# Sorting edges on one core: counts of a group kept in DRAM, order within a column by a rising line and Sign, bias rows of the experts made ahead of their loop

## The chip, the cores and the metric

The kernel runs on one core of a Trainium2 chip. The metric is device time in microseconds (us) of the whole program, the median of several executions; lower is better. A core has five engines with a queue of instructions each: TensorE (PE, matrix products; PEld is its loading of the stationary matrix), VectorE (DVE), ScalarE (ACT), GpSimd (POOL) and SyncE (SP, which here only starts DMAs). Engines work in order within their queue and wait for one another by semaphores. On-chip memory is SBUF (128 partitions) and, for the results of matmuls, PSUM. POOL starts the indirect DMAs, which gather or scatter 128 rows by a list of indices.

## What is computed

A graph layer over 3125 nodes (256 wide), a four-layer transformer with linear attention over the same nodes, and a mixture of four experts routed by a graph attention:

```python
xn = _layernorm(x)
x = x + gnn(xn, edge_attr_64, src, dst, ...) + mix(xn[None], ...)[0]
x = x + ffn(_layernorm(x)[None], ..., L0_ffn_edge_index)[0]

# gnn: messages of 103125 edges (dst is sorted), summed at the receiver, then an MLP
messages = concatenate([nodes[senders], edges], -1) @ W_message
agg = segment_sum(messages, receivers, num_segments=3125)
...
# ffn: attention over 65536 edges (not sorted) and a loop at each node
e = leaky_relu(a_src[src] + a_dst[dst], 0.2)
ee = exp(e - segment_max(e, dst)[dst])
alpha = ee / (segment_sum(ee, dst)[dst] + 1e-16)
agg = segment_sum(h[src] * alpha[:, :, None], dst) + b_gat
scores = _layernorm(agg, ...).reshape(M, 4, 4).mean(1)
topk_s, topk_i = top_k(scores, 2); w = softmax(topk_s)
for ei in range(4):
    g = where(topk_i == ei, w, 0).sum(-1)
    out = out + g[..., None] * (gelu(x @ W1[ei] + b1[ei]) @ W2[ei] + b2[ei])
```

The segment sums and maxima of the last part need the 65536 edges in the order of their receiver, so the kernel sorts them. That sort is what most of the change is about.

## The kernel before

**Layout.** The nodes are 25 tiles of 128 rows, in chunks of four tiles. The 65536 edges to be sorted lie as 128 partitions x 512 columns (TE); a group is 8 columns (GC), so there are 64 groups. A receiver number is cut in two digits: `lo`, its low five bits (32 values), and `hi`, the rest (up to 128 values). A place in the sorted list is: the number of edges with a smaller receiver, plus those with the same receiver in an earlier column, plus those with the same receiver in the same column and an earlier partition.

**Count pass** (`count_group`, L664 to L667, 64 jobs). DVE makes one-hot tiles of both digits with one comparison each (`one_hot`, L657: 128x1024 for `hi`, 128x256 for `lo`). For each column PE multiplies the two (L667) and adds all 512 products up in one PSUM table of 128 x 32 (`table`, part of `sums_ps`): how many edges there are of each receiver. `starts` (L677 to L691) turns the table into the first place of each receiver, which is stored to DRAM (`start_d`) and split into two fp16 parts, `near` and `rest` (`split`, L671 and L672), since one fp16 number can't hold it.

**Place pass** (`place_group`, L693 to L740, 65 jobs: a group's last step, the look, is done one job late). For each group:
1. SP loads `hr`, the high digits of the group's edges broadcast to all partitions (L698, two buffers); DVE compares them with the partition number: `ohT` (L700), the one-hot transposed.
2. DVE makes both one-hots again (L657). PE puts `rest` into column 0 of a PSUM tile (identity x `rest`, L705) and the counts of the eight columns beside it (L707).
3. DVE runs a scan along the columns (L709), PSUM to SBUF: `run`, the start of each receiver at each column. `base` (L712) is the state after the group and is split anew (L671, L672), for the next group.
4. For the order within a column PE puts a mask (identity x `mask`, 0 for a smaller partition and -1 otherwise, L720) into PSUM and adds `ohT` x `ohT` (L722); ACT's Relu (L723) leaves 1 where an earlier partition has the same high digit: `earlier`.
5. One job later PE adds up `ohT` x `near`, `ohT` x `run` and `earlier` x `oh_lo` (the look, 24 matmuls, L734); DVE picks each edge's own value by its low one-hot (L736, L737). Every fourth group `laid` turns 32 columns of numbers into `place`.

POOL then scatters each edge's source to its place (`send`, L750, 512 scatters), and later reads the sorted list.

**What sets the order of the work around it.** The sort is done beside other work. `jobs` is a list of closures with an estimated time, and `beside(us)` (L766) runs the next ones when the transformer's code grants it time: the count groups within layer 0, the ends of the message sums next, the place groups spread over layers 1 to 3. Throughout that time POOL gathers the rows of the message edges (L467, 806 gathers of 128 rows into three buffers `m_run`), DVE adds them up along a partition (L479), and SP stores a full buffer (`run_d`, L484) and loads the edge attributes for the next use of that buffer (L446). Within these bounds a scheduler orders the instructions of each queue; the order in the queues is fixed when the program is built. SP's queue holds all of the loads and stores named here, so each stands behind those ahead of it.

**Experts** (`expert`, L1271). For each of four experts the weights are loaded, then `bias_rows` (L139 to L152) makes the output bias ready for a matmul: a load of the bias to 65 partitions, a fill with zeros and eleven small operations on DVE, which split the fp32 bias into three bf16 rows. Its tiles have one buffer each for all experts. PE adds the bias by a matmul with ones (L1290). Beside the experts POOL gathers the sorted edges' rows (L1192) and DVE works on them in chunks.

Of the kernel before, what the change touches and what calls it, by code (L numbers as in the profile page):

```python
# [18 lines left out]
P = 128  # L19
# [23 lines left out]
GC = 8  # L43
SRC = 4096
# [13 lines left out]
def kernel(ctx: ExitStack, tc: tile.TileContext, a: dict, out: bass.AP):  # L58
# [80 lines left out]
    def bias_rows(pool, vec, name, **k):  # L139

        full = pool.tile([65, D], F32, name=f"{name}_full", **k)
        nc.sync.dma_start(full, vec.rearrange("(o n) -> o n", o=1).to_broadcast([65, D]))
        parts = pool.tile([65, 2, D], BF16, name=f"{name}_parts", **k)
        part = pool.tile([65, D], BF16, name=f"{name}_part", **k)
# [191 lines left out]
    V.tensor_copy(hi, d)  # L336
    hi_f = tmp2.tile([P, TE], F32, name="hi_f")
    V.tensor_copy(hi_f, d)
# [18 lines left out]
    mask = const.tile([P, P], F16, name="mask")  # L357
    V.tensor_scalar(mask, before, -1.0, None, op0=ALU.add)
# [17 lines left out]
    sums_ps = px.tile([P, LO + 2 * NT], F32, name="sums_ps")  # L376

    table, whole_ps, first_ps = sums_ps[:, :LO], sums_ps[:, LO:LO + NT], sums_ps[:, LO + NT:]
# [282 lines left out]
    def one_hots(t):  # L661
        return one_hot(t, hi, P, "oh_hi", 2), one_hot(t, lo, LO, "oh_lo", 3)

    def count_group(t):  # L664
        ohh, ohl = one_hots(t)
        for i in range(GC):
            T.matmul(table, ohh[:, :, i], ohl[:, :, i], start=t + i == 0, stop=t + i == TE - 1, skip_group_check=True)  # L667

    def split(x, near, rest):

        V.tensor_copy(near, x)  # L671
        V.tensor_tensor(rest, x, near, op=ALU.subtract)  # L672

    def parts():
        return (so.tile([P, LO], F16, name="near", bufs=3), so.tile([P, LO], F16, name="rest", bufs=2))

    def starts():  # L677
        cnt2 = so.tile([P, LO], F32, name="cnt2", tag="base")
        V.tensor_copy(cnt2, table)
# [10 lines left out]
        places.append(parts())  # L690
        split(cum2, *places[0])  # L691

    def place_group(t):  # L693

        late = looks.pop() if looks else None
        if t < TE:
            hr = so.tile([P, GC, P], F16, name="hr", bufs=2)
            nc.sync.dma_start(hr.rearrange("p t e -> p (t e)"), row_h[t // GC:t // GC + 1, :].to_broadcast([P, P * GC]))  # L698
            ohT = so.tile([P, GC, P], F16, name="ohT", bufs=2)
            V.tensor_scalar(ohT, hr, bin_p, None, op0=ALU.is_equal)  # L700
            ohh, ohl = one_hots(t)
            near, rest = places.pop()

            cnt = pg.tile([P, LO, GC + 1], F32, name="ps_g")
            T.matmul(cnt[:, :, 0], ident_h, rest, start=True, stop=True)  # L705
            for i in range(GC):
                T.matmul(cnt[:, :, i + 1], ohh[:, :, i], ohl[:, :, i], start=True, stop=True)  # L707
# [9 lines left out]
            for i0 in range(0, GC, 4):  # L717
                ps = pt.tile([P, 4, P], F32, name="ps_t")
                for i in range(4):
                    T.matmul(ps[:, i, :], ident_h, mask, start=i == 0, stop=False, skip_group_check=True)  # L720
# [819 lines left out]
```

## Time and profile before

| what | us |
| --- | --- |
| median of the runs shown (3718.54 to 3738.28) | 3732.21 |
| the profiled execution: time | 3741.95 |
| the profiled execution: span, first to last instruction | 3740.2 |
| PE busy, 10851 matmuls | 2260.1 (60%) |
| POOL busy | 1782.3 (48%) |
| DVE busy | 1478.6 (40%) |
| ACT busy | 1028.8 (28%) |
| message gathers, L467, x806 | 802.7 busy, 996 ns each |
| scatters of the sort, L750, x512 | 494.2 busy, 965 ns each |
| row gathers beside the experts, L1192, x400 | 382.1 busy, 955 ns each |
| sum-ups of the messages, L479, x805 | 437.6 busy, 544 ns each |

A row of a group of instructions reads: line, engine, operation, what it writes and reads by the program's names, the shape, how many; then the busy time and the mean duration of one in ns; then how long the engine was idle just before these instructions, and what ended most of that time. "issue" is time for which the profile shows no wait, "remote" is a release that it can't name. A row of a stage reads: the window and its length, the busy time of each engine with the number of instructions, the clock that TensorE was granted (1 is full speed), the mean busy share of the 16 DMA engines, and GB/s. Over the span the granted clock was 0.762, and 350.22 MB were moved.

By time: 0 to 45 us is preparation, 45 to about 400 layer 0 with the count groups, up to 2745 the place groups (from about 500), 45 to 1690 the message gathers, 1647 to 2822 the scatters, 2900 to 3610 the experts with the edge chunks.

### The profile page before, as it was taken

What the parts mean: (1) busy time and instruction counts of PE and PEld (TensorE: products, weight loads), DVE (VectorE), ACT (ScalarE), POOL (GpSimd) and SP (SyncE); (2) the same over time, 40 slices, a digit from 0 to 9 for tenths busy, and PEclk for the clock granted to TensorE, in tenths of its full rate; (3) what the DMA queues carried; (4) which work ended last, traced back from release to release, by engine and by line L of the source; (5) the groups of instructions that cost most, each with busy time, mean ns of one, the idle gap of its engine ahead of it and who ended that gap; (6) DMA issues with size and microseconds to landing.
All of it is one profiled execution on the core that took longest, in us unless ns stands there. A gap on an engine that the chain in (4) does not pass through costs nothing. (4 is left out here: it accounts for less than half of the span.)

```text
span 3740.2 us, 33303 instructions
## 1 busy us (share of the span) xinstructions
PE 2260.1 (60%) x10851; PEld 1559.5 (42%) x10851; DVE 1478.6 (40%) x4527; ACT 1028.8 (28%) x1876; POOL 1782.3 (48%) x1843
## 2 busy tenths in 40 slices
PE   4666554676568676565475466548667375756470
PEld 2544333455345455343343354436446143424240
DVE  6656534565544555532232233324422022121127
ACT  4412232233223223222232333213233021212122
POOL 3555453554525544544435524443442746464623
PEclk9877776787778787777787777768788677777685
DMA  6566456566635556622010002101100101010101
GB/s 211 188 198 206 136 170 128 178 201 192 212 112 186 174 177 206 203 96 60 20 31 19 20 23 58 35 22 34 35 11 7 16 17 30 14 29 15 27 12 36
DMA packets 282209, 350.22 MB, mean 94 GB/s; under 512 B 178495, under 2 KB 229574, under 8 KB 269222
## 3 DMA queue, kind: packets, MB, share of 16 engines
q1 hardware_dynamic: 211318, 232.55, 19.6%
q0 software_dynamic: 70704, 115.42, 12.1%
q8 instruction: 88, 1.44, 0.2%
q14 instruction: 99, 0.81, 0.1%
HBM read 197.19 MB, written 150.63 MB: 93 GB/s over the span
## 5 line engine op out<-in xcount | busy, mean ns | idle before, releaser
L467 POOL DMA_INDIRECT m_run<-xn_d,src_i x806 | 802.7, 996 | 839.0 <-issue 235.5
L750 POOL DMA_INDIRECT by_dst<-pairs,place x512 | 494.2, 965 | 284.4 <-issue 154.6
L1192 POOL DMA_INDIRECT rows_c<-tab_d,si x400 | 382.1, 955 | 303.0 <-DVE rows_c L1250 184.1
L479 DVE SCALAR_TENSOR_TENSOR m_run<-m_run,stay 128x320 f32<-128x320 f32 x805 | 437.6, 544 | 24.2 <-DMA m_run<-xn_d,src_i 10.4
L1082 PE MATMUL ps_a<-h,w 128*128 128x512 f32 (+1 forms) x896 | 403.0, 592 | 50.0 <-ACT gT L1083 29.2
L1093 PE MATMUL ps_a<-w,gT 128*128 128x256 f32 x1600 | 384.8, 395 | 22.6 <-issue 22.2
L1093 PEld LDWEIGHTS ps_a<-w,gT 128*128 128x128 f32 x1600 | 315.6, 199 | 80.4 <-issue 33.6
L1282 PE MATMUL ps_a<-hT,we 128*128 128x512 f32 (+1 forms) x448 | 228.5, 641 | 170.9 <-issue 92.1
L1082 PEld LDWEIGHTS ps_a<-h,w 128*128 128x128 f32 x896 | 167.6, 207 | 211.5 <-issue 146.6
L1293 PE MATMUL ps_t<-we,hf 128*128 128x256 f32 x800 | 202.8, 406 | 75.2 <-issue 56.0
L1282 PEld LDWEIGHTS ps_a<-hT,we 128*128 128x128 f32 x448 | 90.4, 215 | 322.0 <-issue 227.6
L1293 PEld LDWEIGHTS ps_t<-we,hf 128*128 128x128 f32 x800 | 160.9, 204 | 121.4 <-issue 74.8
L1083 ACT ACTIVATE gT<-ps_a,b 128x512 f32<-128x512 f32 (+1 forms) x224 | 141.2, 641 | 251.3 <-PE ps_a L1082 136.9
L548 POOL DMA_INDIRECT aggr<-run_d,sum_i x25 | 24.4, 975 | 332.5 <-PE ps_t L574 285.3
L598 PE MATMUL ps_a<-gh,gw 128*128 128x256 f32 (+1 forms) x312 | 96.8, 459 | 137.1 <-ACT gh L164 55.2
L723 ACT ACTIVATE earlier<-ps_t 128x512 f16<-128x512 f32 x128 | 71.7, 594 | 381.0 <-PE ps_t L722 218.1
L1242 DVE COPY rows_c<-ev 128x104 f32<-128x104 f32 (+1 forms) x16 | 4.6, 288 | 415.0 <-ACT ev L1204 369.0
L159 PE MATMUL ps_t<-ident,hn 128*128 128x128 f32 x450 | 86.4, 329 | 133.2 <-ACT hn L122 80.9
L1020 PE MATMUL ps_g<-xm,kr 128*128 128x256 f32 x400 | 125.8, 455 | 67.2 <-issue 34.8
L122 ACT ACTIVATE hn<-xm,rstd 128x256 f32<-128x256 f32 x225 | 120.7, 591 | 116.4 <-DVE rstd L118 91.4
L598 PEld LDWEIGHTS ps_a<-gh,gw 128*128 128x128 f32 x312 | 69.8, 238 | 159.0 <-ACT gh L164 56.4
L1020 PEld LDWEIGHTS ps_g<-xm,kr 128*128 128x128 f32 x400 | 86.6, 227 | 112.2 <-ACT kr L1018 52.4
(393 smaller groups left out, 3768.7 us busy)
## 6 DMA issues: line engine op xcount, KB each, us to landing
run_d<-m_run SPq DMA_DIRECT2D x100, 1280.0 KB
m_run<-in_edge_attr_dram SPq DMA_DIRECT2D x95, 256.0 KB
hr<-row_h SPq DMA_DIRECT2D x64, 256.0 KB
m_run<-xn_d,src_i POOLq DMA_INDIRECT x806
w<-in_L_mix_W_dram SPq DMA_DIRECT2D x8, 1024.0 KB
by_dst<-pairs,place POOLq DMA_INDIRECT x512
rows_c<-tab_d,si POOLq DMA_INDIRECT x400
run_d<-rows_c SPq DMA_DIRECT2D x15, 312.0 KB
```

Of the source, the lines that this page charges most:

```text
L122: S.activation(dst, src, AF.Identity, bias=r[:, 1, i:i + 1], scale=r[:, 0, i:i + 1])
L467: last_gather[0] = G.indirect_dma_start(out=m[:, t, :D], out_offset=None, in_=xn_d, in_offset=bass.IndirectOffsetOnAxis(ap=src_i[:, t0 + t ...
L479: add = V.scalar_tensor_tensor(m[:, t, :], before_m, stay[:, c:c + 1], m[:, t, :], op0=ALU.mult, op1=ALU.add)
L598: T.matmul(ps[:, :w], gw[i][:, kc, m * P:(m + 1) * P], h[:, kc, :w], start=kc == 0, stop=kc == 1)
L750: i = G.indirect_dma_start(out=by_dst, out_offset=bass.IndirectOffsetOnAxis(ap=place[:, t:t + 1], axis=0), in_=pairs0[:, t:t + 1], in_offs ...
L1020: T.matmul(ps_x[:, m, :], kr[:, m * P:(m + 1) * P], xm[:, t, :], start=i == 0 and m == 0, stop=i == len(c) - 1, skip_group_check=True)
L1082: T.matmul(ps[:, :w], ff_w[l]["w1"][:, kc, f * P:(f + 1) * P], h2[:, kc, :w], start=kc == 0, stop=kc == 1)
L1083: S.activation(gT[:, f, :w], ps[:, :w], AF.Gelu, bias=ff_w[l]["b1"][:, f:f + 1])
L1093: T.matmul(ps[:, i, :], gT[:, f, (2 * i0 + i) * P:(2 * i0 + i + 1) * P], ff_w[l]["w2"][:, f, :], start=False, stop=f == FF // P - 1, skip_ ...
L1192: G.indirect_dma_start(out=rows_c[:, t - COLS[j], :], out_offset=None, in_=tab_d, in_offset=bass.IndirectOffsetOnAxis(ap=si[:, t:t + 1], a ...
L1282: T.matmul(ps[:, :w], we1[:, kc, f * P:(f + 1) * P], hT[:, kc, c[0] * P:c[0] * P + w], start=kc == 0, stop=kc == 1)
L1293: T.matmul(ps[:, i, :], hh[f][:, (i0 + i) * P:(i0 + i + 1) * P], we2[:, f, :], start=False, stop=f == FF2 // P - 1, skip_group_check=True)
```

## The change

**The count pass** writes each group's eight count products to a PSUM tile of its own (`ps_g`, two buffers, eight columns apart from one another), ACT copies it into an SBUF tile `counts` (two fixed ones, with room for a ninth column ahead of the eight), and SP stores that tile to DRAM, 128 x 576 bytes a group. The table is added up by one matmul a group, identity x counts, 256 columns wide, one job later; `starts` sums its eight parts.

**The place pass** no longer makes the high one-hot or multiplies counts. It loads a group's stored counts into `run` (three buffers; the load is written in the job of the group before), `rest` is written straight into column 0 of that tile by DVE, and the scan works in place in SBUF. For the order within a column partition 127 of the two fixed `ohT` tiles holds a ramp over the edges, 0.25 + e/1024, written once; the one-hots fill the other 127 partitions with the value 2 (so `hi` is clamped to 126). `ohT` x `ohT` then has, beside 4 for the same high digit, a term that rises with the other edge's number; ACT's Sign, with a scale and a bias for each partition, gives +1 or -1 by which side of its own number an edge is on. The look gets a 25th matmul (`all_h`, ones, x the low one-hot, 256 columns), the own value gets another constant, and every fourth group the numbers are halved.

**The experts' bias rows** are made for all four ahead of the expert loop, in buffers of the sort's tiles, with one shared buffer for the loaded bias.

The diff, cut to its core:

```diff
-    def bias_rows(pool, vec, name, **k):
+    def bias_rows(pool, vec, name, tags=(None, None, None)):
...
-    V.tensor_copy(hi, d)
+    V.tensor_scalar(hi, d, float(P - 2), None, op0=ALU.min)
...
-    mask = const.tile([P, P], F16, name="mask")
-    V.tensor_scalar(mask, before, -1.0, None, op0=ALU.add)
+    all_h = const.tile([P, P], F16, name="all_h")
+    V.memset(all_h, 1.0)
+    slope = const.tile([P, 3], F32, name="slope")
+    V.tensor_scalar(slope[:, 0:1], bin_p, 1.0 / 1024, 0.25, op0=ALU.mult, op1=ALU.add)
...
+    ohTs = [so.tile([P, GC, P], F16, name=f"ohT{k}") for k in range(2)]
+    ramp = const.tile([P, P], F16, name="ramp")
+    V.tensor_scalar(ramp, ids, 1.0 / 1024, 0.25, op0=ALU.mult, op1=ALU.add)
+    for o in ohTs:
+        nc.sync.dma_start(o[P - 1:P, :, :], ramp[P - 1:P, :].rearrange("p (o e) -> p o e", o=1).to_broadcast([1, GC, P]))
...
-    sums_ps = px.tile([P, LO + 2 * NT], F32, name="sums_ps")
+    sums_ps = px.tile([P, LO * GC + 2 * NT], F32, name="sums_ps")
...
+    counts_d = dram.tile([GROUPS, P, LO * (GC + 1)], F16, name="counts_d")
+    counted = []
+    cnts = [so.tile([P, LO, GC + 1], F16, name=f"counts{k}") for k in range(2)]
...
     def count_group(t):
-        ohh, ohl = one_hots(t)
-        for i in range(GC):
-            T.matmul(table, ohh[:, :, i], ohl[:, :, i], start=t + i == 0, stop=t + i == TE - 1, skip_group_check=True)
+        if t < TE:
+            ohh, ohl = one_hot(t, hi, P, "oh_hi", 2), one_hot(t, lo, LO, "oh_lo", 3)
+            ps = pg.tile([P, LO, GC], F32, name="ps_g")
+            for i in range(GC):
+                T.matmul(ps[:, :, i], ohh[:, :, i], ohl[:, :, i], start=i == 0, stop=i == GC - 1, skip_group_check=True)
+            cnt = cnts[t // GC % 2]
+            S.copy(cnt[:, :, 1:], ps)
+            nc.sync.dma_start(counts_d[t // GC, :, :], cnt.rearrange("p l i -> p (l i)"))
+            counted.append((t, cnt))
+        if t:
+            t, cnt = counted.pop(0)
+            T.matmul(table, ident_h, cnt[:, :, 1:], start=t == 0, stop=t + GC == TE, skip_group_check=True)
 
     def split(x, near, rest):
         V.tensor_copy(near, x)
-        V.tensor_tensor(rest, x, near, op=ALU.subtract)
+        V.tensor_tensor(rest[:, :, 0], x, near, op=ALU.subtract)
 
-    def parts():
-        return (so.tile([P, LO], F16, name="near", bufs=3), so.tile([P, LO], F16, name="rest", bufs=2))
+    def parts(t):
+        cnt = so.tile([P, LO, GC + 1], F16, name="run", bufs=3)
+        nc.sync.dma_start(cnt.rearrange("p l i -> p (l i)"), counts_d[t // GC, :, :])
+        return (so.tile([P, LO], F16, name="near", bufs=3), cnt)
...
-        V.tensor_copy(cnt2, table)
+        V.tensor_reduce(cnt2, table.rearrange("p (l i) -> p l i", i=GC), AX.X, ALU.add)
...
-            ohT = so.tile([P, GC, P], F16, name="ohT", bufs=2)
-            V.tensor_scalar(ohT, hr, bin_p, None, op0=ALU.is_equal)
-            ohh, ohl = one_hots(t)
-            near, rest = places.pop()
-            cnt = pg.tile([P, LO, GC + 1], F32, name="ps_g")
-            T.matmul(cnt[:, :, 0], ident_h, rest, start=True, stop=True)
-            for i in range(GC):
-                T.matmul(cnt[:, :, i + 1], ohh[:, :, i], ohl[:, :, i], start=True, stop=True)
-            run = so.tile([P, LO, GC + 1], F16, name="run", bufs=2)
+            ohT = ohTs[t // GC % 2]
+            V.tensor_scalar(ohT[:P - 1], hr[:P - 1], bin_p[:P - 1], 2.0, op0=ALU.is_equal, op1=ALU.mult)
+            ohl = one_hot(t, lo, LO, "oh_lo", 3)
+            near, run = places.pop()
             V.tensor_tensor_scan(run.rearrange("p l i -> p (l i)"), goes.rearrange("p l i -> p (l i)"),
-                                 cnt.rearrange("p l i -> p (l i)"), 0.0, op0=ALU.mult, op1=ALU.add)
-            base = so.tile([P, LO], F32, name="base")
-            V.tensor_tensor(base, run[:, :, GC], near, op=ALU.add)
-            places.append(parts())
-            split(base, *places[0])
+                                 run.rearrange("p l i -> p (l i)"), 0.0, op0=ALU.mult, op1=ALU.add)
+            if t + GC < TE:
+                base = so.tile([P, LO], F32, name="base")
+                V.tensor_tensor(base, run[:, :, GC], near, op=ALU.add)
+                places.append(parts(t + GC))
+                split(base, *places[0])
...
                 for i in range(4):
-                    T.matmul(ps[:, i, :], ident_h, mask, start=i == 0, stop=False, skip_group_check=True)
-                for i in range(4):
-                    T.matmul(ps[:, i, :], ohT[:, i0 + i, :], ohT[:, i0 + i, :], start=False, stop=True, skip_group_check=True)
-                S.activation(earlier[:, i0:i0 + 4, :], ps, AF.Relu)
+                    T.matmul(ps[:, i, :], ohT[:, i0 + i, :], ohT[:, i0 + i, :], start=i == 0, stop=i == 3, skip_group_check=True)
+                S.activation(earlier[:, i0:i0 + 4, :], ps, AF.Sign, bias=slope[:, 2:3], scale=slope[:, 1:2])
...
             look = pg.tile([P, GC, LO], F32, name="ps_g")
+            T.matmul(look.rearrange("p i l -> p l i"), all_h, ohl, start=True, stop=False, skip_group_check=True)
...
-                        a1, a2 = ohT[:, i, :], run[:, :, i] if k else near
+                        a1, a2 = ohT[:P - 1, i, :], run[:P - 1, :, i] if k else near[:P - 1]
...
-            V.scalar_tensor_tensor(own, look, E2 / 2, ohl.rearrange("p l i -> p i l"), op0=ALU.add, op1=ALU.mult)
+            V.scalar_tensor_tensor(own, look, float(E2), ohl.rearrange("p l i -> p i l"), op0=ALU.add, op1=ALU.mult)
             V.tensor_reduce(number[t // SG % 2][:, t % SG:t % SG + GC], own, AX.X, ALU.add)
             if (t + GC) % SG == 0:
+                V.tensor_scalar_mul(number[t // SG % 2], number[t // SG % 2], 0.5)
...
-    jobs = [(1.0, lambda t=t: count_group(t)) for t in range(0, TE, GC)]
+    jobs = [(1.0, lambda t=t: count_group(t)) for t in range(0, TE + GC, GC)]
...
-        be2 = bias_rows(ex, a["L0_ffn_b2"][e], "be2")
+        be2 = be2s[e]
...
+    be2s = [bias_rows(so, a["L0_ffn_b2"][e], f"be2{e}", tags) for e, tags in enumerate((
+        ("own_bin", "lo", "base"), ("own_bin", "hi", "base"), ("own_bin", "place", "base"), ("own_bin", "ohT0", "base")))]
     work = (w for e in range(NEXP) for w in expert(e))
```

## Prediction

> **What bounds the kernel now.** I read the page first, then the busy time of each engine by stage, then the groups of the lines that the diff touches (shapes kept apart), then the queue's waits. The followed chain is no help: it breaks off after 2% of the span. No engine is full: PE 60%, POOL 48%, DVE 40%, ACT 28%. By stage (columns: length, then PE, PEld, DVE, ACT and POOL busy with counts, granted clock, DMA share, GB/s):
>
> ```profile
> 45.00:410.00 365.00, 238.79 (x1281) 173.55 (x1281) 220.90 (x560) 106.75 (x197) 203.16 (x198) 0.79 0.58 183
> 500.00:1690.00 1190.00, 769.87 (x4076) 542.81 (x4077) 594.59 (x1572) 343.74 (x639) 569.68 (x578) 0.77 0.55 170
> 1690.00:2900.00 1210.00, 744.37 (x3931) 535.59 (x3929) 368.07 (x1159) 364.73 (x667) 515.39 (x534) 0.77 0.11 28
> 2900.00:3610.00 710.00, 421.46 (x1252) 248.52 (x1251) 132.25 (x696) 139.91 (x216) 386.96 (x405) 0.74 0.13 21
> ```
>
> The count groups lie in the first row, the place groups in the second and third, the experts in the fourth. In no row does any engine pass 66%: the engines take turns, and what lies between is stretches in which POOL issues one indirect DMA after another and nothing else moves. Two of them, in the same columns:
>
> ```profile
> 598.00:622.00 24.00, 2.78 (x11) 1.35 (x12) 0.00 (x0) 0.00 (x0) 15.48 (x17) 0.58 0.44 139
> 2123.00:2157.00 34.00, 0.00 (x0) 0.00 (x0) 1.97 (x6) 0.68 (x2) 21.23 (x22) 0.50 0.03 5
> ```
>
> In the second, PE issues nothing for 34 us, DVE 6 instructions, ACT 2. Counted in the trace, all other engines stand still in such stretches for 516 us in all. The POOL transfers are untouched, so neither are those stretches, unless their places shift. The groups of the lines touched:
>
> ```profile
> L657 DVE TENSOR_TENSOR oh_hi<-bins,hi 128x1024 f16<-128x1024 f16 x128 | 87.2, 682 | 56.3 <-remote 26.1 <-issue 13.8 <-PE ps_a L1082 5.1
> L723 ACT ACTIVATE earlier<-ps_t 128x512 f16<-128x512 f32 x128 | 71.7, 594 | 381.0 <-PE ps_t L722 218.1 <-remote 116.5 <-PE ps_g L734 14.7
> L720 PE MATMUL ps_t<-mask,ident_h 128*128 128x128 f16 x512 | 54.9, 234 | 12.1 <-issue 8.6 <-ACT earlier L723 2.8 <-DVE h L609 0.4
> L709 DVE TENSOR_TENSOR_SCAN run<-goes,ps_g 128x288 f16<-128x288 f16 x64 | 47.9, 748 | 156.3 <-remote 85.8 <-PE ps_a L598 33.5 <-PE ps_a L994 16.9
> L707 PE MATMUL ps_g<-oh_lo,oh_hi 128*128 128x32 f16 x512 | 46.5, 241 | 28.8 <-issue 18.0 <-DVE oh_lo L657 10.8
> L705 PE MATMUL ps_g<-rest,ident_h 128*128 128x32 f16 x64 | 13.5, 210 | 107.3 <-DVE rest L672 94.0 <-issue 11.9 <-DVE own_bin L736 1.3
> L164 ACT ACTIVATE h<-ps_t,b1n,g 128x512 f32<-128x512 f32 x48 | 34.8, 772 | 43.1 <-remote 31.2 <-issue 8.3 <-PE ps_t L159 2.9
> L401 PE MATMUL ps_a<-dst_h,ends_buf 128*128 128x403 f16 x50 | 18.8, 460 | 26.3 <-DVE xm L1096 10.4 <-issue 10.2 <-ACT ends_buf L403 4.0
> ```
>
> To be seen: what goes is some 115 us of PE's 2260 and 44 us of DVE's 1479, and before L705 and L709 stands idle time larger than their work.
>
> **PE.** Removed in the place pass: 512 count matmuls (L707), 512 mask matmuls (L720), 64 of L705. Their busy times are 46.5 + 54.9 + 13.5 = 115 us, but these overlap one another: counted in the trace, eight L707 start in 0.65 us and four of 128 columns in 0.40, some 0.06 us apiece when they run back to back, so 1088 x 0.06 = 65 us. I take the 65, as these come in bursts. Added: one matmul of 256 columns per group in each pass, 128 in all. A 256-column one costs between two steps of the 128-column row (0.12 us) and L401's 460 ns x 256/403 = 0.29; nearer to the bursts, 0.16, so +20 (15 to 37). Net -45 us (-100 to -28).
>
> **DVE.** Removed: 64 high one-hots, 64 x 0.682 = -43.6. Added: 16 halvings of 32 columns at 0.17 (the 32-column cast of L671, mean 174 ns) = +3; a second operation in ohT and a scan reading SBUF in place of PSUM, at 0 to 7 together, taken as 0 because L700 already takes 493 ns for 1024 elements and L709 is serial. Net -41 (-44 to -33).
>
> **ACT.** Added: 64 copies of 128x256 out of PSUM; the row of the same shape (L1025, x8) says 0.376 us, so +24. Sign has pointers for bias and scale where Relu had constants: L164, 512 columns with both pointers, 772 ns against 594, so 128 x 0.18 = +23; the lower bound is 0, as L403's Sign with a bias pointer takes 598 ns. Net +47 (24 to 47).
>
> **What reaches the end.** A microsecond off an engine that is busy in turns counts for a share. For 500 to 2900 us the rows sum to PE 1514, DVE 963, ACT 708: shares .475, .30 and .22. So -45 x .475 = -21, -41 x .30 = -12, +47 x .22 = +10: **-23**. The estimate is coarse, and its bounds are -100 x .475 - 44 x .30 + 24 x .22 = -55 and -28 x .475 - 33 x .30 + 47 x .22 = -13.
>
> **Waits that go.** The scan no longer follows PE, nor PE (L705) the rest of the group before. Of L705's 94.0 us, two waits of 34.7 and 30.4 end at 2157 and 2522, the ends of stretches such as the second one above; there PE would stop at its next need of DVE or ACT anyway. That leaves 29 us. What is late next is ohT for L722 (30.2 us already) and own_bin on DVE (L736, idle 150.2). I take half, **-15** (0 to -100; the far end is under the first rival).
>
> **Waits that come.** In the place pass `rest` is written into the loaded counts, so DVE's L672 waits for a load by SP; behind it on DVE stand the next ohT, one-hots and the sum-ups (L479). The load needs only a free buffer of three, so it can be issued a group ahead, as hr's is; at nothing, then. Without that cover it is about 4.8 us (issue of own_n's load to the DVE operation that reads it, 643.96 to 648.72), 64 x 4.8 = 307 us of DVE, at .30 some +92. In the count pass, SP's store waits for ACT's copy, that for the eight matmuls: 0.65 + 0.376 = 1.0 us. Behind it in SP's queue stand the run_d stores (L484) and attribute loads (L446), and behind these POOL's gathers. How much of SP's waiting POOL feels:
>
> ```profile
> SPq L484 <- DVE m_run L479: 424.8, 44, 37.4
> SPq L446 <- DMA run_d<-m_run: 195.7, 46, 8.7
> SPq L698 <- DVE ohT L700: 173.6, 19, 50.0
> POOL m_run L467 <- DMA run_d<-m_run: 126.4, 10, 40.6
> ```
>
> (waited for: us in total, times, longest). 126.4 of 424.8 + 195.7 is .20. So 64 x 1.0 x .20 = **+13** (0 to +66). The table matmul comes a group late, so PE does not wait for it. The added bytes, 2 x 64 x 73.7 KB = 9.4 MB, are 2.7% of 350 MB where DMA stands at .58 and less: nothing, or +9.4 MB / 183 GB/s = 51 us x .58 = 30 if wholly exposed.
>
> **Expert bias rows.** Now L145 to L151 wait inside each expert until the one before has ended: DVE 3098.98 to 3101.82, then PE's L1290 at 3101.88, after 2.67 us idle. Three such turns at 2.9 us go: **-9**. The far end is L145's idle time, -57 (56.7 us, DVE's, mostly wanted by nobody). Moved ahead of the experts, four rounds share a buffer, each a load that waits for the DVE of the round before, 4 x (4.8 + 2.8) = 30 us, and the last needs the buffer of `place`, free after the last scatter near 2822. SP's loads for finish (L785) may stand behind them. Experts start near 2900, so this is covered; if half were not, +15.
>
> **Two rules weighed.** The rows first: TensorE's clock was .67 in 2200 to 2300 with PE busy 52 of 100 us, .86 in 2800 to 2900 with 77. The sum holds the clock as it is, since span and PE work shrink together. By the rows' slope, 45/3740 = 1.2% less busy would cost .009 of clock and 2260 x .009/.762 x .475 = +13 us. The Trainium skill ("TensorE: Matmul & The Clock Gate", Part 1: The HAM clock gate) says that an idle window halves the clock, so fewer matmuls could mean slower ones; by it the +13 would stand. Second, gathers beside the sum-ups, which read two SBUF tensors, take 996 ns, rows_c gathers with little DVE work 955: 806 x .041 = 33 us for 438 us of such DVE work, and for the scan's 47.9 us that is 4. The sum has 0. The Trainium skill ("SBUF — State Buffer", Who interferes with whom) says that a DVE operation with both inputs in SBUF shuts out a GpSimd operation that reads SBUF; the scan becomes such a one, and by the rule that is up to 48 us.
>
> **Sum.** -23 - 15 - 9 + 13 = -34. The profiled execution took 3741.95 (span 3740.2 and 1.75 around it), 9.7 over the median 3732.2; the gain is put on the median: **3698**. Its own range is 3665 (the engines' far end, -55) to 3713 (the first price of a slower case, +15).
>
> **Rivals.** (1) DVE comes free of PE and the waits really go: 94 + 156 = 250 us, of which 1 - .60 counts because PE is busy .60 of the span: -100 in place of -15, so 3613. For it: the longest waits of the place pass lie on these two lines. Against: 85.8 of the 156.3 are idle "remote", in the POOL stretches. (2) No change, 3732: the 34 us are swallowed in stretches whose length POOL sets (1794 indirect DMAs at 1.25 us are 2240 us of the span). For it: the 516 us; against: they are not full and PE's queue is longer than POOL's. (3) Slower, by SP's queue: the counts' load and store hold SP as hr's load now does. L698 is waited for 412.7 us by the rows of SP (173.6 on ohT, 239.1 on rest, near, base and others), 6.4 us a group; 64 x 6.4 x .20 = +82 over run_d and the gathers, so 3732 - 34 + 82 = 3780. It decides from 34/(64 x .20) = 2.7 us a group. For it: SP has one queue and hr's long holds; against: a buffer more for the counts, and in the count pass the writer is short. The late load above gives +92, the same size, 3790.
>
> **Chances.** Forecast .45, larger gain .07, no change .15, slower .33. What a measurement of this kernel can tell from no change is 0.5%, 19 us. Faster .52, same .15, slower .33. The range reaches from 3645, which is 3698 less 32 for the engines' far end and about half of the bias rows' far end, to 3795, just over the two prices of the slower case; the larger gain stays outside.
>
> **What would show it.** Right: L657's oh_hi x64, no L720, L707, L705; the scan without idle on PE; Sign near 0.77; PE some 45 to 100 us less busy; L1290 with no DVE ahead of it. Slower case: SP waiting on ACT for the counts or on PE for a free buffer, and POOL's wait on run_d over 126 us. Late load: DVE's rest waiting on the counts' DMA for over 2 us a group. Wrong altogether: the idle stretches beside POOL moving by more than 40 us in total, since the sum holds them fixed.

## The result, and the profile after

The changed kernel takes 3719.91 us (median of 20 runs) where the kernel before takes 3726.06 (20 runs): ratio 0.9975, 95% interval 0.9952 to 0.9997. That is 9 us (1 to 18) where 34 were forecast: a gain, but within the 0.5% that the prediction called no change; the two medians by themselves are 6 us apart. The profiled execution took 3726.91, its span 3725.2, against 3740.2.

The chips turned out to be of two kinds. In the runs of the result, and on two chips that later runs fell on, the kernel before takes 3726 to 3778 us; on four others it takes 2541 to 2547. The document calls them the **first** and the **second kind**; every ratio compares runs on one chip. On the second kind the same change makes the kernel 1.8% slower. What makes a chip one or the other, no run tells. Both answers are needed to see what the prediction got right.

First the page of the kernel after on the first kind, part 1, and its stages (columns as before):

```profile
PE 2232.7 (60%) x9891; PEld 1505.7 (40%) x9891; DVE 1452.2 (39%) x4484; ACT 1062.2 (29%) x1933; POOL 1776.0 (48%) x1843
45.00:410.00 365.00, 237.90 (x1245) 170.27 (x1244) 210.81 (x514) 119.17 (x244) 191.44 (x190) 0.79 0.60 189
500.00:1690.00 1190.00, 767.97 (x3585) 523.84 (x3584) 587.73 (x1581) 367.95 (x663) 587.21 (x598) 0.77 0.56 177
1690.00:2900.00 1210.00, 739.08 (x3507) 516.79 (x3506) 366.28 (x1182) 365.23 (x661) 523.94 (x542) 0.77 0.12 30
```

PE has 27 us less than before, DVE 26 less, ACT 33 more. In these stages of equal length PE is as busy as before (238, 768 and 739 us against 239, 770 and 744): the stages are as full as they were. The count products begin later, at 198 us in place of 50, and end at 434 in place of 398; the message gathers end at 1638, before at 1647, and the experts begin 12 us earlier, at 2882. The groups that answer to those shown of before, with the one of before that is not shown yet ahead of them:

```profile
L736 DVE SCALAR_TENSOR_TENSOR own_bin<-ps_g,oh_lo 128x256 f32<-128x256 f32 x64 | 38.5, 602 | 150.2 <-remote 112.4 <-PE ps_t L159 14.9 <-issue 14.6
L668 DVE TENSOR_TENSOR oh_hi<-bins,hi 128x1024 f16<-128x1024 f16 x64 | 43.5, 686 | 69.8 <-PE ps_g L683 29.1 <-issue 17.8 <-remote 14.8
L741 ACT ACTIVATE earlier<-ps_t,slope 128x512 f16<-128x512 f32 x128 | 93.8, 773 | 260.0 <-PE ps_t L740 146.2 <-remote 98.6 <-PE ps_g L753 8.8
L728 DVE TENSOR_TENSOR_SCAN run<-goes,run 128x288 f16<-128x288 f16 x64 | 48.1, 751 | 0.6
L746 PE MATMUL ps_g<-oh_lo,all_h 128*128 128x256 f16 x64 | 28.9, 451 | 20.5 <-issue 9.8 <-DVE oh_lo L668 8.9 <-DVE laid L657 1.6
L690 PE MATMUL sums_ps<-counts,ident_h 128*128 128x256 f16 x64 | 20.4, 318 | 39.4 <-issue 29.4 <-ACT counts L685 9.8
L685 ACT CAST counts<-ps_g 128x256 f16<-128x256 f32 x64 | 22.7, 372 | 92.3 <-issue 33.2 <-PE ps_g L683 25.6 <-DMA counts_d<-counts 22.4
L755 DVE SCALAR_TENSOR_TENSOR own_bin<-ps_g,oh_lo 128x256 f32<-128x256 f32 x64 | 38.2, 596 | 244.2 <-remote 198.0 <-PE ps_a L1101 23.1 <-PE ps_a L1090 12.5
L695 DVE TENSOR_TENSOR run<-base,near 128x32 f16<-128x32 f32 x63 | 18.5, 294 | 50.2 <-DMA run<-counts_d 49.8
L694 DVE CAST near<-base 128x32 f16<-128x32 f32 x63 | 12.1, 191 | 49.7 <-remote 37.8 <-PE ps_a L1101 7.4 <-issue 3.6
```

Read the middle figures first: half of the high one-hots are gone, Sign takes 773 ns, the copy of the counts 372, as expected (772, 376). The 256-column matmuls take 451 and 318 ns, where 160 were put. Then the idle times: the scan, 156.3 us idle before, now has 0.6; but own_bin has 244.2 in place of 150.2, and `rest` (L695) and `near` (L694) 50 each, in place of nothing. The wait went one step on, not away: in all DVE stands idle 2273 us after and 2262 before, PE 1493 and 1480. In the queues' waits (waited for: us in total, times, longest):

```profile
SPq L699 <- remote: 258.8, 16, 38.2
SPq L699 <- PE ps_g L753: 186.7, 26, 37.8
SPq L686 <- ACT counts L685: 82.8, 34, 18.6
SPq L723 <- DVE ohT L725: 119.4, 12, 53.7
POOL m_run L478 <- DMA run_d<-m_run: 50.4, 15, 13.3
```

SP now stands 445 us before the load of the counts (L699) and 83 before their store (L686), as the slower rival said. With all smaller rows of the lines that handle counts and `hr` it is 778 us (L699 515, L686 83, L723 180) against 455 at `hr` before (L698). But SP's waits as a whole did not grow, 2990 us against 2999: it waits less elsewhere, at the stores of run_d above all (422 us against 541). What POOL waits for those stores fell from 126.4 to 50.4 us, but all of its idle time before the gathers is about the same, 839.0 us before and 835.9 after:

```profile
L467 POOL DMA_INDIRECT m_run<-xn_d,src_i x806 | 802.7, 996 | 839.0 <-issue 235.5
L478 POOL DMA_INDIRECT m_run<-xn_d,src_i x806 | 797.5, 989 | 835.9 <-issue 228.2
```

So SP's holds made POOL's waits before the gathers neither longer nor shorter.

### The profile page after: what moved, and what is told of

Same layout as the page of the kernel before. It is cut to its first block, busy times and chain, and to the rows that moved or that the text cites. A ratio compares the mean times of both kernels' runs of the same rounds, so it can differ in the third digit from the quotient of the medians.

```text
span 3725.2 us, 31745 instructions
## 1 busy us (share of the span) xinstructions
PE 2232.7 (60%) x9891; PEld 1505.7 (40%) x9891; DVE 1452.2 (39%) x4484; ACT 1062.2 (29%) x1933; POOL 1776.0 (48%) x1843
## 3 DMA queue, kind: packets, MB, share of 16 engines
q1 hardware_dynamic: 229782, 242.00, 20.4%
## 5 line engine op out<-in xcount | busy, mean ns | idle before, releaser
L478 POOL DMA_INDIRECT m_run<-xn_d,src_i x806 | 797.5, 989 | 835.9 <-issue 228.2
L1101 PE MATMUL ps_a<-h,w 128*128 128x512 f32 (+1 forms) x896 | 413.0, 604 | 101.5 <-ACT gT L1102 38.5
L1112 PE MATMUL ps_a<-w,gT 128*128 128x256 f32 x1600 | 382.3, 394 | 20.4 <-issue 19.9
L609 PE MATMUL ps_a<-gh,gw 128*128 128x256 f32 (+1 forms) x312 | 106.4, 489 | 207.7 <-DVE gh L612 95.8
L741 ACT ACTIVATE earlier<-ps_t,slope 128x512 f16<-128x512 f32 x128 | 93.8, 773 | 260.0 <-PE ps_t L740 146.2
```

The source lines that it names most:

```text
L478: last_gather[0] = G.indirect_dma_start(out=m[:, t, :D], out_offset=None, in_=xn_d, in_offset=bass.IndirectOffsetOnAxis(ap=src_i[:, t0 + t ...
L609: T.matmul(ps[:, :w], gw[i][:, kc, m * P:(m + 1) * P], h[:, kc, :w], start=kc == 0, stop=kc == 1)
L1101: T.matmul(ps[:, :w], ff_w[l]["w1"][:, kc, f * P:(f + 1) * P], h2[:, kc, :w], start=kc == 0, stop=kc == 1)
L1112: T.matmul(ps[:, i, :], gT[:, f, (2 * i0 + i) * P:(2 * i0 + i + 1) * P], ff_w[l]["w2"][:, f, :], start=False, stop=f == FF // P - 1, skip_ ...
```

## Experiments

Each kernel ran beside the kernel before on the same chip. Ratios are to the kernel before, with their 95% intervals. before_again, named below, is a trace of the kernel before on the second kind.

| kernel | kind | before, us | ratio | interval |
| --- | --- | --- | --- | --- |
| after (the result) | first | 3726 | 0.9975 | 0.9952 to 0.9997 |
| after_again | second | 2541 | 1.0182 | 1.0158 to 1.0207 |
| counts_only | second | 2546 | 0.9959 | 0.9944 to 0.9975 |
| counts_only2 | second | 2547 | 0.9977 | 0.9966 to 0.9988 |
| sign_only | second | 2546 | 1.0012 | 0.9999 to 1.0026 |
| sign_only2 | second | 2547 | 1.0019 | 1.0009 to 1.0029 |
| bias_only | second | 2541 | 1.0147 | 1.0119 to 1.0176 |
| bias_only2 | second | 2545 | 1.0124 | 1.0105 to 1.0144 |
| bias_late | second | 2546 | 0.9949 | 0.9932 to 0.9965 |
| bias_free | first | 3738 | 0.9948 | 0.9916 to 0.9980 |
| bias_free2 | first | 3778 | 0.9975 | 0.9938 to 1.0012 |
| bias_free3 | second | 2547 | 0.9956 | 0.9938 to 0.9974 |
| mask_x4 | second | 2546 | 1.0084 | 1.0066 to 1.0102 |
| mask_x8 | first | 3778 | 1.0439 | 1.0383 to 1.0496 |
| high_x4 | second | 2541 | 1.0170 | 1.0148 to 1.0193 |
| high_x8 | first | 3778 | 0.9956 | 0.9915 to 0.9997 |
| relu_x4 | second | 2547 | 1.0216 | 1.0199 to 1.0234 |
| relu_x8 | second | 2545 | 1.0875 | 1.0855 to 1.0895 |

### What a microsecond of each engine counts

The prediction gave work of the place pass shares of .475 (PE), .30 (DVE) and .22 (ACT). Doing one operation several times measures them.

```diff
-                for i in range(4):
-                    T.matmul(ps[:, i, :], ident_h, mask, start=i == 0, stop=False, skip_group_check=True)
+                for k in range(4):      # mask_x4; 8 in mask_x8
+                    for i in range(4):
+                        T.matmul(ps[:, i, :], ident_h, mask, start=k + i == 0, stop=False, skip_group_check=True)
```

> The kernel before with the mask product of the place pass issued four times in place of once (1536 more matmuls of 128 columns; the order within a column comes out the same). By the row of before this is 3 x 54.9 = 165 us more of busy PE, 92 us if they start 0.06 us apart. Theory A (the prediction's shares: a microsecond of PE in the place pass counts .475): +44 to +78 us on the kernel before, ratio 1.012 to 1.021. Theory B (work of the place pass lies under other work or under the stretches that POOL sets): under +15 us, ratio below 1.004.

> The kernel before with the mask product of the place pass issued eight times: 3584 more matmuls, 7 x 54.9 = 384 us busy by the row of before, 215 us at 0.06 us apiece. Theory A (PE counts .475): +102 to +182 us. Theory B (work of the place pass lies under other work): mask_x4 cost 21 us for 165 busy, .13, where before takes 2546 us, so +50. On a chip where before takes 3730 us, where all engines stand still for some 500 us beside POOL: +20 to +50 if what the engines do between the stretches is not what sets the time; +150 or more if POOL and the other engines really alternate, since then every added microsecond is in turn.

mask_x4 fell on the second kind: 2570.41 against 2545.95, +24 by the medians and +21 by the ratio. Its PE is busy 2117.8 us against 2047.7 in a trace of before on that kind (below), so +70, and the share is 21/70 = .30. mask_x8 fell on the first kind:

```profile
PE 2493.1 (63%) x14435; PEld 1772.6 (45%) x14435; DVE 1498.2 (38%) x4527; ACT 1033.8 (26%) x1876; POOL 1772.1 (45%) x1843
```

2493.1 - 2260.1 = 233 us more of PE, and .0439 x 3778 = 166 us (145 to 187) of time: **.71 of PE's added busy time counts** there. The figure is a rough one: no trace of before is from that chip, and the rows of the mask products alone grew by 269 us (323.6 against 54.9), so with both spreads it is .54 to .80. So on the second kind theory B is the nearer. On the first neither is: PE's work counts more than its share, and the +150 or more that was expected if POOL and the other engines alternate is met.

```diff
             ohh, ohl = one_hots(t)
+            for k in range(3):          # high_x4; 7 in high_x8
+                V.tensor_tensor(ohh, bins, hi[:, t:t + GC].rearrange("p (o t) -> p o t", o=1).to_broadcast([P, P, GC]),
+                                op=ALU.is_equal)
```

> The kernel before with the high one-hot of the place pass made four times: 192 more DVE operations of 0.682 us, 131 us of DVE, and PE's count matmuls that much later. Theory A (a share of .30 for DVE): +39 us. Theory B (POOL's chain of indirect DMAs sets the time, other work costs only where POOL waits for it): as in mask_x4, where 165 us of PE cost 21 us, .13 of it, so +10 to +20 us.

> The kernel before with the high one-hot of the place pass made eight times: 7 x 43.6 = 305 us more of DVE. Theory A (DVE counts .30): +92 us. high_x4 cost 45 us for 131 (.34) where before takes 2541 us, so +104 there. On a chip where before takes 3730 us: +92 by A; +300 if POOL and the other engines alternate; under +50 if the stretches take it up.

high_x4, on the second kind, costs 43 us for 131 us of added one-hots, .33 (.40 of the 108 us that DVE is busy longer): near the share of .30, but not for its reason. What got longer are POOL's own instructions; before_again first, then high_x4:

```profile
L467 POOL DMA_INDIRECT m_run<-xn_d,src_i x806 | 819.6, 1017 | 334.0 <-issue 219.7
L467 POOL DMA_INDIRECT m_run<-xn_d,src_i x806 | 851.5, 1056 | 339.1 <-issue 213.3
```

The scatters take 1015 ns in place of 990, and POOL is busy 1862.8 us against 1819.5: +43, the whole cost. POOL's waits (its gaps of over 0.5 us, counted in the traces) are 174 us against 166. high_x8, on the first kind:

```profile
PE 2282.6 (61%) x10851; PEld 1575.0 (42%) x10851; DVE 1734.1 (46%) x4975; ACT 1029.7 (27%) x1876; POOL 1844.7 (49%) x1843
```

DVE is busy 1734.1 us against 1478.6, 255 more, and the time is not longer: by the ratio 17 us shorter (1 to 32), by the medians of all runs 4. **DVE's added work in the place pass counts nothing there.** The gathers are longer here too (1058 ns against 996, POOL 62 us busier), but POOL's waits are shorter, 1368 us against 1424. "Under +50 if the stretches take it up" is what was met.

```diff
-                S.activation(earlier[:, i0:i0 + 4, :], ps, AF.Relu)
+                for _ in range(4):      # relu_x4; 8 in relu_x8
+                    S.activation(earlier[:, i0:i0 + 4, :], ps, AF.Relu)
```

> The kernel before with each Relu of the place pass done four times into the same tile: 384 more of 594 ns on ACT, 215 us by the row of before. The prediction's share of .22: +47 us. On a chip where before takes about 3740 us, PE's added work counted .71 of its busy time there (mask_x8: +166 us for +233) and DVE's nothing (high_x8): if ACT counts as PE does, +150; if nothing, as DVE, within 15. What is left of the sum of after there is -27 x .71 = -19 us of PE against -9 measured, so a share near .3 would close it: +65 us. On a chip where before takes 2541 us: +45 to +90, by the shares of .31 (PE) and .42 (DVE) there.

> The kernel before with each Relu of the place pass done eight times: 896 more of 594 ns on ACT, 502 us. On a chip where before takes 2547 us relu_x4 cost 54 us for 215 (.25), so +125 or somewhat more. On a chip where before takes about 3740 us: +150 by a share of .3 (which would close the sum of after), +356 if ACT counts .71 as PE's busy time does there, under 15 if nothing, as DVE's.

Both fell on the second kind. ACT is busy 192 and 441 us more (1218.8 and 1467.8 against 1026.9), the time is 55 and 223 us longer: .29 and .51, near the share at first and well over it then, also over the "+125 or somewhat more" that was expected. What ACT counts on the first kind stays open.

On the second kind all of these costs are seen at POOL, whose indirect DMAs, with gaps of up to 1 us, fill 2332 us of the span of 2538: its waits are 166 us before, 197 in mask_x4 (+31), 231 in relu_x4 (+65) and 410 in relu_x8 (+244), while in high_x4 its instructions are longer. So work of the other engines costs time there as far as it makes POOL wait, or makes POOL's own instructions longer.

### The parts alone

counts_only is before with the diff's count pass, `parts` and the scan in place (the one-hot of the high digits and nine matmuls a group gone), sign_only is before with the ramp, Sign and the 25th look matmul. In counts_only the bias rows stay within the experts.

> The kernel before with the counts kept in DRAM alone: mask and Relu stay, the experts' bias rows stay late (in buffers of the sort). By the rows of after, PE loses 46.5 + 13.5 and gains 20.4 (-40 us busy), DVE loses 43.6 and gains 7 on rest, ACT gains 22.7. Theory A with nothing given back: -40 x .475 - 37 x .30 + 23 x .22 = -25 us, ratio .993. Theory A with the gain given back by what the loads and stores hold up in SP's queue: 0 to +20 us, ratio 1.000 to 1.005. Theory B: within 10 us, and SP's long waits at the counts' load without effect.

> The kernel before with the ramp and Sign alone: counts are multiplied again in the place pass, bias rows stay late. PE loses 54.9 (31 at the pitch) and gains 28.9 for the look's 256-column matmul (451 ns in after), ACT gains 128 x 0.18 = 23. Theory A: between -26 x .475 + 23 x .22 = -7 and -2 x .475 + 5 = +4 us, so ratio .998 to 1.001. Theory B: 0. If it is faster by over 15 us, both are wrong and the mask products cost more than their row.

> The counts in DRAM alone, again, beside the same runs of before as Sign alone. On a chip where before takes about 3740 us: PE loses 46.5 + 13.5 - 20.4 = 40 us busy, times .71 = -28, DVE's 37 us count nothing, ACT's +23 at .3 are +7: -21 us, ratio .994. If the waits for the counts' load (SP 446 us at L699 in after) cost something: 1.000 or more. On a chip where before takes 2541 us: .996 as before.

> Sign and the ramp alone, again. On a chip where before takes about 3740 us: PE loses 54.9 and gains 28.9 (-26 us, or -2 at the pitch of back-to-back matmuls) times .71 = -18 to -1, ACT +23 at .3 = +7: -11 to +6 us, ratio .997 to 1.002. On a chip where before takes 2541 us: 1.001 as before.

All four fell on the second kind: by the ratios the counts in DRAM gain 6 to 10 us, and the ramp and Sign lose 3 to 5 (the first of the two runs within its noise). Sign trades PE's 54.9 us for 28.9 of the look's new matmul and 23 us more of ACT, which comes out a little worse than even; that these two make the loss is the likely reason, not a shown one. Which of the two parts makes the gain on the first kind is not measured.

bias_only is before with the early bias rows (the fourth set in a buffer of its own, for want of the fixed ohT tile); bias_late is after with the rows made within each expert again.

> The kernel after with the bias rows made inside each expert again (in buffers of the sort, one for all experts, so that each waits for the expert before). The prediction's -9 us would show as +9 over after, so a ratio to the kernel before of .9999; if the wait is covered by the loading of the weights, which also waits for the expert before, it stands at after's .9975; if the early rounds delayed the start of the experts, it is below .9975.

> The kernel before once more, for a trace on the chip of the experiments. If the chip is of the kind of the first four experiments (2546 us): span near 2545, POOL idle (gaps over 0.5 us between its instructions) under 200 us in all, PE, DVE and ACT idle together for under 110 us. If it is of the kind of the profile before: span near 3730, POOL idle near 1420 us, all three idle together over 500 us.

> The kernel after, unchanged, beside the same runs of before as the other three. Parts measured alone gave counts .9959, Sign 1.0012, and after with late bias rows .9949. If the parts add up and the early bias rows are worth -9 us, .991 to .992; if the early bias rows are worth nothing, .995. On a chip of the kind of the profile before, .9975 again.

> The kernel before with the early bias rows alone. The prediction's term: -9 us (.9975 on a time near 3700, .9965 on one near 2546). If the start of the experts waits for the four rounds: +15 us. If PE's wait for the bias at the head of an expert is covered by POOL's row gathers: 0.

> The kernel before with the early bias rows alone, once more. On a chip where before takes about 3740 us: within 10 us of it (.997 to 1.003), since DVE stands still beside the scatters there anyway, and the fill of the third set waits in that time. On a chip where before takes 2541 to 2547 us: 1.0147 as before.

On the second kind the early bias rows alone cost 1.47% and 1.24%, 37 and 32 us, and after without them is .9949 (on another chip of that kind): all of after's loss is theirs. after_again was expected at .991 to .995; even the parts measured alone would make only 1.012, and it has 1.0182. before_again shows where it is lost. A wait of POOL in the stage in which the last chunks are finished (1800 to 1960 us), first before, then bias_only:

```profile
POOL tgt_d L812 <- DVE tab L805: 12.5, 2, 9.5
```

```profile
POOL tgt_d L811 <- DVE tab L804: 44.2, 3, 34.1
```

The target scatters wait for `tab` 44.2 us in place of 12.5. bias_only's timeline shows why (some of its rows: start, length, engine, line, operation; in brackets the idle time before it and what ended it), DVE first, then SP:

```profile
1831.63 0.29 DVE L146 CAST be_part<-be_full 65x256 bf16<-65x256 f32 x1 [1.71 <-DMA be_full<-in_L_ffn_b_dram]
1870.51 0.27 DVE L144 MEMSET be_parts<- 65x256 uint32 x1 [38.14 <-DMA by_dst<-pairs,place]
```

```profile
1829.42 43.54 SPq L143 DMA_DIRECT2D be_full<-in_L_ffn_b_dram  x2
1876.06 0.39 SPq L808 DMA_DIRECT2D tab_d<-tab  x1
```

The zero fill of the third set (L144) goes into the buffer of `place`, free after the last scatter. DVE stands 38 us before it; SP, whose next load of the shared bias buffer waits for DVE, stands 43 us; the stores of `tab` and the last loads of the finish stand behind it in SP's queue. The next store of `tab` starts at 1843 in before, here at 1876. In after_again DVE's wait at the same fill is 56.9 us.

### One buffer moved

```diff
-        ("own_bin", "lo", "base"), ("own_bin", "hi", "base"), ("own_bin", "place", "base"), ("own_bin", "ohT0", "base")))]
+        ("own_bin", "lo", "base"), ("own_bin", "hi", "base"), ("own_bin", "earlier", "base"), ("own_bin", "ohT0", "base")))]
```

(and two buffers for the tag `earlier`, as it has elsewhere.)

> The kernel after with one word changed: the third set of bias rows lies in a buffer of the order tiles (free after the last look) and not in that of the places (free after the last scatter). Theory C, from bias_only and after on a chip where before takes 2541 us (DVE stood 38 us at the fill of the third set, SP 43 to 62 us behind it, POOL's target scatters 34 us): the wait is all that the early bias rows cost, so this kernel comes to .9949 - .0035 = .991, at most .9949, where after had 1.0182. If the four loads in a row are what holds SP, it stays at 1.010 or more. On a chip where before takes 3726 us, before stands still in that stretch anyway (DVE 40 us), so .995 to .998 as after.

> The kernel after with the third set of bias rows in a buffer of the order tiles, again, since the run before fell on a chip where the kernel before takes 3738 us (ratio .9948). On a chip where before takes 2541 us: .991 to .995 if the wait for the places is all that early bias rows cost there, 1.010 or more if the four loads in a row are. On a chip as the last: .9948 again, between .992 and .998.

> The kernel after with the third set of bias rows in a buffer of the order tiles, once more, for a chip where before takes 2541 us: .991 to .995 there if the wait for the places is all that early bias rows cost, 1.010 or more if the four loads in a row are. On a chip where before takes about 3740 us: .994 to .999, as the two runs before.

On the second kind this takes after from 1.0182 to .9956 (.9938 to .9974): 57 us, as long as that wait, and nothing is left over: the one wait is the whole cost. It does no better than bias_late (.9949), so early bias rows gain nothing there. PE's waits for them at the head of an expert, 58.7 us in before_again (before the matmul L1290, three turns), are gone in bias_free3, but POOL's row gathers take the same 510 us (1916 to 2427 before, 1913 to 2423).

On the first kind bias_free gives .9948 and .9975, after .9975: no cost of the wait can be told there, though by an estimate from the three intervals there is room for up to 18 us. DVE in that stage shows a reason (a line of its waits between 2755 and 2900 us), for before, after and bias_free:

```profile
DVE tab L800 <- PE ps_g L799: 50.0, 12, 40.2
```

```profile
DVE be_parts L145 <- DMA by_dst<-pairs,place: 29.4, 1, 29.4
```

```profile
DVE tab L819 <- remote: 24.2, 1, 24.2
```

There DVE stands still anyway while POOL issues the last scatters: 40.2 us in before behind PE's L799, 24.2 in bias_free for a release that the profile can't name. After's 29.4 us for the places stand in the same gap: in each of the three traces this idle time ends within 6 us of the start of the last scatter.

bias_free is the version to keep: it beats both kernels on the second kind, and on the first its ratio is below 1 in both runs (in one beyond its interval; in the other the medians are 4 us the other way), though not told apart from after.

## Why the prediction was wrong

**The sum, term by term, on the first kind.** *PE, -45 us:* mis-sized. Removed were the rows named, but the two 256-column matmuls were put at 0.16 us, nearer to two steps of the 128-column row (0.12) than to L401's scaled 0.29; they measured 0.451 and 0.318, outside those bounds, 28.9 + 20.4 = 49 us in place of 20. PE's busy time fell by 27 us. *PE's share, .475:* this is PE's part of what PE, DVE and ACT are busy together; of the 2400 us of the two stages it is .63. mask_x8 says .71 (.54 to .80) of the busy time, so -19 us of time (-15 to -22) if work taken away counts as work added does. That this is near the -21 forecast is luck: the two errors cancel. *DVE, -41 x .30 = -12:* DVE's busy time fell by 26 us; by its rows it is 33 (one-hots -43, halvings +3, `rest` +7, at 294 ns in place of 184). high_x8 says that added DVE work counts nothing there, so the term is put at 0. *ACT, +47 x .22 = +10:* +33 measured in busy time; its share is not measured there. *Waits that go, -15:* the waits on the two lines went, and stand at own_bin, near and rest; DVE and PE are idle in all no less than before (2273 and 1493 us against 2262 and 1480). The prediction named own_bin as next, and still booked half. *Bias rows, -9:* experts took 722 us before (2894.0 to 3616.2) and 719 after, so -3 at most. *Waits that come, +13:* SP's holds at the counts came, larger than assumed, but SP's waits as a whole and POOL's idle time before the gathers stayed as they were, so 0.

What is left is -19 for PE; with ACT at the prediction's share, 33 x .22 = +7, the sum is -12 (-15 with the experts' 3) against -9 (-18 to -1) measured. That fits, but ACT's share there is argued and not measured, and the fit is not proof. Between the two profiled executions, 15 us apart, POOL's busy time is 6 us shorter (gathers 989 ns against 996) and its waits 8; high_x4 and high_x8 show that the high one-hots lengthen POOL's DMAs, and 64 of them are gone. That term is not in the prediction's sum, and no run separates it from PE's. *Clock:* 0.762 in both profiles, with PE busy 60% of the span in both, so the +13 of the rows' slope did not come. Nor is there the lower clock that fewer matmuls could have brought by the Trainium skill ("TensorE: Matmul & The Clock Gate", Part 1: The HAM clock gate), which says that an idle window halves the clock.

So the core of the mechanism, less PE work in the place pass, which does count, was not what failed. The steps that failed are three gains beside it that were booked and did not come: DVE's share (-12, measured as nothing), the waits that go (-15, they moved on) and the bias rows (-9, at most 3). Against them stands the +13 of SP's queue, which did not come either.

**The signs.** Those of the forecast came (no L720, L707 and L705, the scan without idle time on PE, Sign at 773 ns, no DVE ahead of the bias matmul) but for PE, 27 us less busy where 45 to 100 were named. Of the slower case SP's waits came and POOL's longer wait on run_d did not. The late load came in part: `rest` waits 49.8 us for the counts, 0.8 us a group, under the 2 named. The idle stretches beside POOL, which the sum holds fixed, are 533 us after and 518 before (PE, DVE and ACT still for over 6 us at a time), so that assumption held.

**The rivals.** "No change", .15, is what by its bound took place, but not for its reason: the gain was not swallowed by POOL's stretches, since PE's work counts .71. The slower rival had the wait right (SP at the counts' load) and its price wrong: SP's holds at the counts' load and store and at hr come to 778 us after against 455 before (the 413 of the prediction leave out small rows), 5.1 us a group more and over its point of 2.7, yet POOL felt none of it. The share of .20, POOL's waits over SP's, was taken from totals and is no price of one more hold.

**What is slower elsewhere.** The prediction saw the four rounds, the shared buffer, and that the last scatter frees the place; it put +15 for half of 30 us uncovered and called it covered because experts start near 2900. The cover was wrongly named: what the wait delays is the finish stage ahead of the experts, by way of SP's queue. On the first kind DVE's standstill beside the scatters is the likely cover, as the lines of that stage have it; without it, on the second, the price is 32 to 37 us for the early rows alone and 57 in the kernel after.

## What to carry to other kernels

A share of the path that an engine gets from its busy time is a guess; one kernel that does the operation four or eight times measures it, and may show that 255 us more of an engine cost nothing. Look then also at what the other engines' instructions take: 131 us more of DVE cost 43 on the second kind, by way of POOL's. When work is moved ahead into borrowed buffers, ask of each buffer who frees it last, and what stands behind the waiting instruction in the other queues: here one of four buffers cost more than all that the rest of the change gained. And name the cover of a wait by what it delays first, not by the stage it was made for.

## What the runs showed of the hardware

The same program takes 2541 to 2547 us on four chips and 3738 to 3778 on two others (3726 in the runs of the result). The page of before_again, on the second kind (part 1, then PE, DVE, ACT, POOL and clock by fortieths of the span):

```profile
PE 2047.7 (81%) x10851; PEld 1466.3 (58%) x10851; DVE 1474.2 (58%) x4527; ACT 1026.9 (40%) x1876; POOL 1819.5 (72%) x1843
PE   3979788688799998796999988999997659595850
DVE  7978877579868767773544537556331222222258
ACT  4633245333344444342545654444442223232322
POOL 3677777677767777767777777777747777777754
PEclk9989788888899999897999989999998879797965
```

Busy times differ by a tenth for PE (the granted clock is 0.894 here and 0.762 on the first kind), and hardly for DVE, ACT and POOL. What differs is whether they run at once. In runs of POOL's indirect DMAs without a gap of over 1 us, beyond their first 10 us, PE is busy .84 of the time on the second kind and .38 on the first, DVE .56 and .16 (counted from the two traces of before); POOL's waits come to 166 us against 1424, and PE, DVE and ACT stand still together (for over 6 us at a time) 92 us against 518. There POOL and the other engines mostly take turns; here they run side by side, and POOL's chain is the bound for most of the span.

The 48 us that the rule of the Trainium skill ("SBUF — State Buffer", Who interferes with whom) would have put on the scan did not show: the gathers took 989 ns after and 996 before. But 64 high one-hots went at the same time, which read two SBUF tensors as well, and these do lengthen the gathers (1017 to 1056 ns in high_x4, for 192 more of them). That agrees with the rule, though the way it comes about is not shown; what the scan by itself adds is not separated.
